# Fetches two steps ahead, mixes a unit later, gate logits behind the branch: a rearranged order in an RNN and mixture attention kernel

## The chip, the cores and the metric

The kernel runs on one core of one Trainium2 chip. The metric is the device time of one execution in microseconds (us); the time of a kernel is the median of its runs. TensorE is called PE, its weight loads PEld, VectorE DVE, ScalarE ACT, GpSimd POOL and SyncE SP. A letter q behind an engine's name in the profile means its sequencer.

## The reference, cut to what matters

Two layers, each with a residual, in float32, for 2 sequences of 2048 tokens of width 256:

```python
h_new = tanh(xi[t] + h @ Wh.T + bh)               # xi = layernorm(x) @ Wi.T + bi, over 2048 steps
x = x + hs
n = layernorm(x)                                  # 8 heads of 64, 5 experts, 2 of them chosen
gl_v = (n @ Ws).reshape(b, t, h, e);  wv = topk_mask(gl_v, 2) * sigmoid(gl_v)
xv = einsum('btd,edk->btek', n, Wv);  v = einsum('bthe,btek->bhtk', wv, xv)
attn = softmax(q * scale @ k.T) @ v               # q = n @ Wq, k = n @ Wk, per head
mask_o = topk_mask((n @ Wd).reshape(b, t, h, e), 2)
out = x + einsum('bthe,bthk,ekd->btd', mask_o, attn, Wo)
```

## The kernel before, in words

**Preparation.** The tokens are held as 16 chunks of 128 (`NCH` and `S` are 16). `measure` computes layer norm statistics on DVE, `turn_in` (L286) normalizes a chunk on POOL, transposes it on PE and copies it on ACT, and `project_in` (L297) multiplies it by Wi. In the loop at L318 `turn_in(c + 1)` is issued ahead of `project_in(c)`.

**The recurrence.** It is run as 128 short pieces side by side, twice (`run("a")` and `run("b")`, 13 and 16 steps); then DVE compares the pieces' ends with their starts (L504 to L509), and a branch on the count (L522, L523) repeats the run if they differ. `beside(s)` (L463) is issued behind each step of the second run: `turn_back` (L384) transposes the states of a chunk on PE and adds them to the residual `xt[c]` (ACT copies to `hv` and POOL adds, L395 and L396; for the last chunk DVE adds straight from PSUM, L392), and `x1d` is stored through SP. Behind the comparison stand `turn_norm` (L451) of the first eight chunks, and `logits` (L481) of chunks 0 to 3, with the matmul of the count, L517, in its middle. Its PSUM tile is of the pool `misc`, which has two buffers. After the branch come `queries(0, 0)`, `keys(0, 0)`, `logits(4)` and `turn_norm` of the other chunks.

**The attention.** There are 16 heads (2 sequences by 8), 4 blocks of 512 queries each: 64 units of four steps, `NT` = 256 steps in all. In step T, PE computes the scores (L634) of two key chunks, ACT copies them to SBUF (`stage`, L645), DVE keeps a running maximum (`largest`, L655). `LAG` = 6 steps later the maximum has been subtracted (`subtract`, L693, six of eight on POOL, the others on DVE), ACT has taken exponentials (L696), and PE multiplies by v (`products`, L706). A DMA issued by POOL adds pairs of probabilities (`fold`, L718).

**The order of the work beside it** is written out by hand. `at(table, T, f)` puts a call into step T, either `before` or `behind` the step's products; a later call for the same T comes later. What matters here:

- `fetch` (L605) loads the five experts' values of four chunks into `xq`, a tile with one buffer of 640 KB, by a DMA on SP's queue. `mix` (L610) multiplies it by the gates (L619), `mix_sum` (L623) sums over experts into `v` (L625). Each head has four parts. For heads after the first, `mix` stands at T, `fetch` at T - 1, `mix_sum` at T + 1 (L944 to L947). For the first head, `mix` reads values that were not fetched (`xf`).
- `experts` (L583) computes the second sequence's values while the first is in attention, two chunks in each of units 20 to 27, copies them (L588) and stores them on SP's queue (L589). The even chunk stands behind step 1 of a unit, the odd one before step 2.
- `gates` (L904) ranks the logits: ACT copies them to a tile of `misc` (`lg`, L223), DVE compares (`lt`, L236), and POOL counts ranks in five calls of `gates_go_on` (L241, L242, and L247 at the end for output gates). For the first sequence the output gates of part 0 and 1 stand at T = 4 and 10 (L925, L927). They are read first by `weigh` in `close` (L768), at step 12 for part 0 and 20 for part 1.

[...]

Of the kernel before, what the change touches and what calls it, by code (L numbers as in the profile page):

```python
# [14 lines left out]
P = 128  # L15
# [5 lines left out]
def rnn_then_switchhead_kernel(  # L21
# [98 lines left out]
    def misc(shape, nm):  # L120
        return ps_m.tile(shape, F32, tag="m", name=nm)
# [148 lines left out]
    with tc.tile_pool(name="prep", bufs=3) as pp, tc.tile_pool(  # L270
        name="lna", bufs=3
    ) as lnp, tc.tile_pool(name="ps_xi", bufs=3, space=PSUM) as ps_xi, tc.tile_pool(
        name="ps_t", bufs=3, space=PSUM
    ) as ps_t, tc.manual_schedule():
        norm_of, turned = {}, {}

        def measure(c0, n):
            mv = pp.tile([P, n * B, 2], F32, tag=f"mv{n}", name=f"mva{c0}")
            for c in range(c0, c0 + n):
                for b in range(B):  # L280
                    stats(lnp, mv[:, (c - c0) * B + b, :], xt[c][:, b, :], f"a{c}_{b}")
            neg, y = scales(lnp, mv, n * B, f"a{c0}")
            for c in range(c0, c0 + n):
                norm_of[c] = neg, y, (c - c0) * B

        def turn_in(c):  # L286
            neg, y, k = norm_of.pop(c)
            xn = pp.tile([P, B, D], F32, tag="xn", bufs=2, name=f"xn{c}")
            tp = ps_t.tile([P, KC, B, P], F32, tag="tp", name=f"tpa{c}")
            for b in range(B):  # L290
                normalize(xn[:, b, :], xt[c][:, b, :], neg, y, k + b)
                for kc in range(KC):
                    nc.tensor.transpose(tp[:, kc, b, :], xn[:, b, kc * P : (kc + 1) * P], ident)
            turned[c] = pp.tile([P, KC, B, P], F32, tag="xnT", bufs=2, name=f"xnT{c}")
            nc.scalar.copy(turned[c], tp)

        def project_in(c):  # L297
            xnT = turned.pop(c)
            for mc in range(KC):
                px = ps_xi.tile([P, B, P], F32, tag="px", name=f"px{c}_{mc}")  # L300
                for kc in range(KC):
                    nc.tensor.matmul(
                        px.rearrange("p b n -> p (b n)"),
                        lhsT=wi[:, kc, mc * P : (mc + 1) * P],
                        rhs=xnT[:, kc].rearrange("p b n -> p (b n)"),
                        start=kc == 0,
                        stop=kc == KC - 1,
                    )
                nc.scalar.activation(xi[:, mc, c], px, AF.Identity, bias=bsum[:, mc : mc + 1])

        groups, c0 = [], 0
        for n in (1, 1, 2, 3, 4, 5):
            groups.append((c0, n))
            c0 += n
        assert c0 == NCH
        measure(*groups.pop(0))
        nc.vector.tensor_tensor(bsum, bias[:, 0, :], bias[:, 1, :], ALU.add)
        for c in range(NCH):  # L318
            while groups and groups[0][0] <= c + 2:
                measure(*groups.pop(0))  # L320
            if c == 0:
                turn_in(0)
                project_in(0)
            if c + 1 < NCH:
                turn_in(c + 1)
            if c:
                project_in(c)


# [15 lines left out]
    ps_t = ctx.enter_context(ExitStack())  # L345
    pst = ps_t.enter_context(tc.tile_pool(name="ps_tb", bufs=2, space=PSUM))
    mv2 = [sp.tile([P, GC, 2], F32, tag=f"mv{g}", bufs=1, name=f"mvb{g}") for g in range(2)]
    tp_of, root_of = {}, {}

    def step(nm, s, prev, h, ps_h):  # L350
        for b in range(B):
# [29 lines left out]
                beside(s)  # L381
            prev = lambda kc, b, h=h: h[:, kc, b, :]

    def turn_back(c, nm, eng=None):  # L384

        tp = pst.tile([P, B, KC, P], F32, tag="tp", name=f"tpb{nm}{c}")
        for b in range(B):
            for kc in range(KC):
                nc.tensor.transpose(tp[:, b, kc, :], hs[:, kc, c, b, :], ident)
        tp = tp.rearrange("p b c d -> p b (c d)")  # L390
        if eng is nc.vector:
            nc.vector.tensor_tensor(xt[c], xt[c], tp, ALU.add)  # L392
        else:
            hv = sp.tile([P, B, D], F32, tag="hv", bufs=2, name=f"hv{nm}{c}")
            nc.scalar.copy(hv, tp)  # L395
            nc.gpsimd.tensor_tensor(xt[c], xt[c], hv, ALU.add)  # L396
        nc.sync.dma_start(out=x1d[c], in_=xt[c])

    def stats_back(c, nm):
# [63 lines left out]
    def beside(s):  # L463
        if s >= 1:
            turn_back(s - 1, "b")
        if s >= 2:
            stats_back(s - 2, "b")
        if s == GC + 2:
            root_of["todo"] = roots(mv2[0], GC, "b")
            next(root_of["todo"])  # L470
            next(root_of["todo"])
        if s == GC + 3:
            next(root_of["todo"])
            next(root_of["todo"])
        if s == GC + 4:
            *_, root_of[0] = root_of["todo"]
        if s >= GC + 4:
            c = 2 * (s - GC - 4)
            xn_of[c] = norm_back(c, "b", (nc.scalar, nc.gpsimd))

    def logits(c0, nm, between=None):  # L481

        pg = misc([P, 4, 2 * HE], f"pg{nm}{c0}")
        for c in range(c0, c0 + 4):
            for kc in range(KC):
                nc.tensor.matmul(
                    pg[:, c - c0, :],
                    lhsT=xn2T[:, kc, 0, c * P : (c + 1) * P],
                    rhs=wsd[:, kc, :],
                    start=kc == 0,  # L490
                    stop=kc == KC - 1,
                )
            if between and c == c0 + 1:
                between()
        nc.scalar.copy(gates_all[:, c0 : c0 + 4, 0, :], pg)

    with tc.tile_pool(name="ps_h", bufs=1, space=PSUM) as ps_h:

        with tc.manual_schedule():
            run("a", True, False, ps_h)  # L500
            run("b", False, True, ps_h, beside)
            N = KC * B * NS
            off = sp.tile([P, KC, B, NS], F32, tag="off", bufs=1, name="off")
            nc.vector.tensor_tensor(off, hs[:, :, S - 1], ends[:, :, :, 1:], ALU.subtract)  # L504
            good = sp.tile([P, KC, B, NS], F32, tag="good", bufs=1, name="good")
            nc.vector.tensor_scalar(good, off, TOL, None, ALU.is_le)
            nc.vector.scalar_tensor_tensor(good, off, -TOL, good, ALU.is_ge, ALU.mult)
            count = sp.tile([P, 1], F32, tag="count", bufs=1, name="count")
            nc.vector.tensor_reduce(count, good.rearrange("p c b n -> p (c b n)"), AX.X, ALU.add)  # L509
            turn_norm(0, xn_of.pop(0), "b")  # L510
            turn_back(S - 1, "b", nc.vector)
            for c in range(2, GC, 2):
                turn_norm(c, xn_of.pop(c), "b")
            pc = misc([1, 1], "pc")
            logits(
                0, "b",
                lambda: nc.tensor.matmul(pc, lhsT=count, rhs=ones, start=True, stop=True),  # L517
            )
            stats_back(EARLY - 1, "b")
            again = sp.tile([1, 1], I32, tag="again", bufs=1, name="again")  # L520
            nc.vector.tensor_scalar(again, pc, float(P * N) - 0.5, None, ALU.is_lt)
        flag = nc.values_load(again[0:1, 0:1], min_val=0, max_val=1)  # L522
        with tc.If(flag > 0):  # L523
            for c in range(S):
                load_x(c)
            with tc.For_i(0, NS - 1, 1):
                nc.vector.tensor_copy(ends[:, :, :, 1:], hs[:, :, S - 1])
                run("c", False, True, ps_h)
            for c in range(S):
                turn_back(c, "c")  # L530
                if c < EARLY:
                    stats_back(c, "c")
            *_, root_of[0] = roots(mv2[0], GC, "c")
            for c in range(0, GC, 2):
                turn_norm(c, norm_back(c, "c", pool2), "c")
            logits(0, "c")

    with tc.manual_schedule():

# [2 lines left out]
        for c in range(GC, S, 2):  # L542
            xn_of[c] = norm_back(c, "d", (nc.vector, nc.gpsimd))
        queries(0, 0)
        keys(0, 0)
        logits(4, "d")
        for c in range(GC, S, 2):
            turn_norm(c, xn_of.pop(c), "d")
    ps_t.close()
# [372 lines left out]
        at(behind, part, logits_first, HC + 4 * part)  # L922
    for part in range(2):
        at(behind, 1 + part, gates, 0, part, 0, True)
        at(behind, 4 + 6 * part, gates, 0, part, 1, False)  # L925
        for k in range(E):
            at(behind, 5 + 6 * part + k, gates_go_on)  # L927
    for i, (b, h) in enumerate(heads):
        T0 = i * H_T
        if i == 0:  # L930
# [8 lines left out]
        for part in range(4):  # L939
# [1 line left out]
                at(behind, (3, 5, 6, 7)[part], mix, i, part)  # L941
                at(behind, (3, 5, 6, 7)[part], mix_sum, i, part)
            else:
                T = max(T0 + U_T * (part - 3) + 2, LAG + 2)  # L944
                at(behind, T - 1, fetch, i, part)
                at(behind, T, mix, i, part)
                at(before, T + 1, mix_sum, i, part)  # L947
        if h == H - 3 and b + 1 < B:
# [158 lines left out]
```

## Time and profile before

| what | us |
|---|---|
| median of 3 runs (lowest, highest) | 1626.83 (1624.53, 1630.81) |
| the profiled execution: its time, its span | 1623.28, 1621.5 |
| PE, DVE, ACT, POOL busy | 1539.0, 1296.5, 1250.2, 1284.8 |
| attention starts (first copy of a score tile) | 135.0 |
| a unit of four steps, late in the span (four units from 1166.5 on) | 19.9, 21.5, 20.9, 20.6 |
| units 0 to 3 | 28.1, 29.3, 27.4, 21.0 |
| units 20 to 27 (584.8 to 782.3) | 197.5 in all |

Busy time of an engine over the whole span is an average over stages; what a change in one stage is worth is read from the windows of that stage. A unit is counted from the first copy L645 of its first step.

### The profile page before, as it was taken

How to read it: one execution, taken by the hardware profiler on the slowest of the kernel's cores; microseconds unless marked ns; L12 is line 12 of the kernel's file. 1: busy time of each engine (PE TensorE's matmuls, PEld its weight loads, DVE VectorE, ACT ScalarE, POOL GpSimd, SP SyncE). 2: the span in 40 equal slices, each digit the busy share in tenths (PEclk: the TensorE clock that was granted, in tenths of full speed). 3: DMA queues.
4: the chain of work that ended last, by engine and by line, in shares of the span. 5: the costliest groups of instructions: out<-in, count | busy, mean ns of one | idle time of the engine just before them, and what ended most of it. 6: DMA issues, size and time to landing. Idle time of an engine off the chain costs nothing.

```text
span 1621.5 us, 29233 instructions
## 1 busy us (share of the span) xinstructions
PE 1539.0 (95%) x11442; PEld 594.1 (37%) x11442; DVE 1296.5 (80%) x1807; ACT 1250.2 (77%) x1616; POOL 1284.8 (79%) x857
## 2 busy tenths in 40 slices
PE   6989899999999999998999999999999999999996
PEld 5974223333333333333333333333333333333333
DVE  7473789998988887777887768898888888988763
ACT  4664678888888888777887768888888888888862
POOL 3054688888888988888998768898889899998980
PEclk9999999999999999999999999999999999999999
DMA  5021368788888888677886767788888888889762
GB/s 161 1 106 37 106 141 193 176 188 173 178 172 172 173 168 172 139 166 143 180 182 156 174 148 178 168 169 174 169 172 169 178 160 177 168 174 186 153 134 86
DMA packets 86624, 252.27 MB, mean 156 GB/s; under 512 B 11920, under 2 KB 31184, under 8 KB 86480
## 3 DMA queue, kind: packets, MB, share of 16 engines
q0 software_dynamic: 43200, 163.60, 53.9%
q1 hardware_dynamic: 41648, 86.13, 17.6%
q8 instruction: 92, 1.51, 0.4%
q10 hardware_dynamic: 1632, 0.61, 0.1%
q14 instruction: 52, 0.43, 0.1%
HBM read 59.46 MB, written 50.33 MB: 68 GB/s over the span
## 4 chain that ended last, share of the span: by engine, by line
PE 64%; DVE 15%; DMA 6%; ACT 3%; issue 3%; POOL 1%; SPq 0%; DVEq 0%; ACTq 0%
PE s L634 23%; PE o L706 20%; DVE m L655 6%; PE d L727 6%; PE pq L159 4%; PE pk L140 3%; ACT p L645 3%; DMA xq<-xvd 2%; DMA p<-p 2%; PE pz L846 2%; DVE pro L772 2%; PE pt L683 2%; PE pm L668 1%; DVE p L693 1%; PE po L759 1%
## 5 line engine op out<-in xcount | busy, mean ns | idle before, releaser
L693 POOL TENSOR_TENSOR p<-p,top 128x1024 f32<-128x1024 f32 x381 | 1053.6, 3002 | 4.8 <-ACT top L686 4.6
L645 ACT COPY p<-s 128x1024 f32<-128x1024 f32 x512 | 511.0, 1011 | 161.4 <-DVE m L655 70.1
L696 ACT ACTIVATE p<-p 128x1024 f32<-128x1024 f32 x512 | 538.1, 1062 | 47.8 <-DVE p L693 38.1
L634 PE MATMUL s<-qs,k 64*128 64x512 f32 x1024 | 511.3, 617 | 7.7 <-ACT p L645 7.7
L634 PE MATMUL s<-q,k 64*128 64x512 f32 x1024 | 511.3, 617 | 6.7 <-ACT p L645 5.9
L706 PE MATMUL o<-p,v 128*32 128x512 f32 x4096 | 492.0, 597 | 8.5 <-DVE os L743 6.4
L655 DVE TENSOR_TENSOR m<-s,m 128x1024 f32<-128x1024 f32 x320 | 390.7, 1221 | 78.3 <-PE s L634 69.1
L718 POOL DMA_DIRECT2D p<-p x252 | 339.8, 1348 | 69.7 <-ACT p L696 22.9
L706 PEld LDWEIGHTS o<-p,v 128*32 128x32 f32 x4096 | 114.6, 109 | 297.2 <-issue 157.7
L634 PEld LDWEIGHTS s<-qs,k 64*128 64x128 f32 x1024 | 168.8, 185 | 145.3 <-issue 49.2
L634 PEld LDWEIGHTS s<-q,k 64*128 64x128 f32 x1024 | 168.8, 185 | 141.9 <-issue 49.6
L693 DVE TENSOR_TENSOR p<-p,pt 128x1024 f32<-128x1024 f32 x131 | 158.4, 1210 | 0.1
L727 PE MATMUL d<-p,ones 128*32 128x512 f32 x1040 | 151.5, 594 | 1.7 <-DMA p<-p 1.7
L655 DVE TENSOR_TENSOR m<-s,p 128x1024 f32<-128x1024 f32 x64 | 78.4, 1224 | 53.8 <-ACT p L645 53.4
L814 POOL DMA_DIRECT2D yd<-pro x48 | 43.3, 903 | 94.1 <-DVE pro L772 90.2
L619 DVE TENSOR_TENSOR xq<-xq,wp 128x1280 f32<-128x1280 f32 x60 | 89.2, 1487 | 28.3 <-DMA xq<-xvd 26.5
L772 DVE TENSOR_TENSOR pro<-po,mr 128x1280 f32<-128x1280 f32 (+1 forms) x67 | 95.9, 1431 | 2.7
L625 DVE TENSOR_REDUCE v<-xq 128x256 f32<-128x1280 f32 x60 | 88.6, 1476 | 0.0
L159 PE MATMUL pq<-xn2T,wq 128*32 128x512 f32 x512 | 66.8, 635 | 12.8 <-DVE xq L619 8.7
L727 PEld LDWEIGHTS d<-p,ones 128*32 128x32 f32 x1040 | 37.8, 110 | 91.9 <-issue 77.0
L140 PE MATMUL pk<-xn2T,wk 128*32 128x512 f32 x512 | 61.5, 598 | 0.7 <-ACT q L169 0.7
L673 DVE TENSOR_REDUCE mq<-pm 128x4 f32<-128x512 f32 x64 | 44.3, 692 | 19.2 <-PE pm L668 17.8
(175 smaller groups left out, 1472.4 us busy)
## 6 DMA issues: line engine op xcount, KB each, us to landing
p<-p POOLq DMA_DIRECT2D x252, 512.0 KB, 6.2
xq<-xvd SPq DMA_DIRECT2D x60, 640.0 KB, 5.2
yd<-pro POOLq DMA_DIRECT2D x48, 640.0 KB, 7.5
qs<-q SPq DMA_DIRECT2D x64, 128.0 KB, 2.7
yd<-pro SPq DMA_DIRECT2D x8, 640.0 KB, 4.1
y<-yd SPq DMA_DIRECT2D x8, 640.0 KB, 6.8
x<-in_x SPq DMA_DIRECT2D x16, 256.0 KB, 5.5
x1d<-x SPq DMA_DIRECT2D x16, 256.0 KB, 2.0
```

The lines of the kernel that those rows point to most:

```text
L140: nc.tensor.matmul(pk[at_col : at_col + 32], lhsT=wk[:, kc, h * DH + g : h * DH + g + 32], rhs=xc[:, kc, c0 // 2 : (c0 + HC) // 2, o, :], ...
L159: nc.tensor.matmul(pq[at_col : at_col + 32, :], lhsT=wq[:, kc, h * DH + g : h * DH + g + 32], rhs=xn2T[:, kc, b, n * QB : (n + 1) * QB], s ...
L619: nc.vector.tensor_tensor(xq, xq, wp.unsqueeze(2).to_broadcast([P, 4, DH, E]), ALU.mult)
L634: nc.tensor.matmul(ss[:, o, :], lhsT=k_of[i][half, c, :], rhs=q_of[i, n][o][half, :], start=True, stop=True,)
L645: nc.scalar.copy(p, ss)
L655: nc.vector.tensor_tensor(m, ss, ring[t - 1] if c == 1 else m, ALU.max)
L693: eng.tensor_tensor(p, p, top.unsqueeze(1).to_broadcast([P, 2, QB]), ALU.subtract)
L696: nc.scalar.activation(ring[t], ring[t], AF.Exp)
L706: nc.tensor.matmul(o_of[u][at_col : at_col + 32, :], lhsT=v_of[i][:, 2 * c + o, g : g + 32], rhs=ring[t][:, o, :], start=c == 0, stop=c == ...
L718: nc.gpsimd.dma_start(out=ring[t], in_=ring.pop(t + 1), accum_op=ALU.add)
L727: nc.tensor.matmul(den_of[u][32 * g : 32 * (g + 1), :], lhsT=ones32, rhs=ring[(t, t1)[g // 2]][:, g % 2, :], start=first, stop=last, tile_ ...
L772: nc.vector.tensor_tensor(dst, po[:, s : s + n, 0:DH].unsqueeze(2).to_broadcast([P, n, E, DH]), mr[:, s : s + n].unsqueeze(3).to_broadcast ...
```

## The change

Six edits, all of order and place:

1. `project_in(1)` is issued ahead of `turn_in(2)`.
2. `turn_back` only transposes and copies to `hv`, for the last chunk too; a new `add_back` adds. The sums of chunks 14 and 15 move to DVE, behind the comparison.
3. `logits(0)` moves from ahead of the branch to behind `queries(0, 0)`, and both `logits` take a PSUM tile of the pool of the transposes instead of `misc`.
4. `turn_norm(0)` follows the last `turn_back`.
5. The output gates of the first sequence move three steps on.
6. Mixes move four steps on (one unit), and each fetch stands two steps ahead of its mix instead of one.

```diff
-                project_in(0)
+            if c < 2:
+                project_in(c)
             if c + 1 < NCH:
                 turn_in(c + 1)
-            if c:
+            if c >= 2:
                 project_in(c)
...
-        tp = tp.rearrange("p b c d -> p b (c d)")
-        if eng is nc.vector:
-            nc.vector.tensor_tensor(xt[c], xt[c], tp, ALU.add)
-        else:
-            hv = sp.tile([P, B, D], F32, tag="hv", bufs=2, name=f"hv{nm}{c}")
-            nc.scalar.copy(hv, tp)
-            nc.gpsimd.tensor_tensor(xt[c], xt[c], hv, ALU.add)
+        hv_of[c] = sp.tile([P, B, D], F32, tag="hv", bufs=2, name=f"hv{nm}{c}")
+        nc.scalar.copy(hv_of[c], tp.rearrange("p b c d -> p b (c d)"))
+
+    def add_back(c, eng):
+
+        eng.tensor_tensor(xt[c], xt[c], hv_of.pop(c), ALU.add)
         nc.sync.dma_start(out=x1d[c], in_=xt[c])
...
         if s >= 1:
             turn_back(s - 1, "b")
+        if 1 <= s < S - 1:
+            add_back(s - 1, nc.gpsimd)
...
-        pg = misc([P, 4, 2 * HE], f"pg{nm}{c0}")
+        pg = pst.tile([P, B * D], F32, tag="tp", name=f"pgd{c0}")[:, : 4 * 2 * HE]
+        pg = pg.rearrange("p (c g) -> p c g", c=4)
...
-            turn_norm(0, xn_of.pop(0), "b")
-            turn_back(S - 1, "b", nc.vector)
-            for c in range(2, GC, 2):
+            turn_back(S - 1, "b")
+            for c in range(0, GC, 2):
                 turn_norm(c, xn_of.pop(c), "b")
             pc = misc([1, 1], "pc")
-            logits(
-                0, "b",
-                lambda: nc.tensor.matmul(pc, lhsT=count, rhs=ones, start=True, stop=True),
-            )
+            nc.tensor.matmul(pc, lhsT=count, rhs=ones, start=True, stop=True)
+            for c in (S - 2, S - 1):
+                add_back(c, nc.vector)
...
         queries(0, 0)
+        logits(0)
         keys(0, 0)
-        logits(4, "d")
+        logits(4)
...
-        at(behind, 4 + 6 * part, gates, 0, part, 1, False)
+        at(behind, 7 + 6 * part, gates, 0, part, 1, False)
         for k in range(E):
-            at(behind, 5 + 6 * part + k, gates_go_on)
+            at(behind, 8 + 6 * part + k, gates_go_on)
...
-                T = max(T0 + U_T * (part - 3) + 2, LAG + 2)
-                at(behind, T - 1, fetch, i, part)
+                T = T0 + U_T * (part - 2) + 2
+                at(behind, T - 2, fetch, i, part)
                 at(behind, T, mix, i, part)
                 at(before, T + 1, mix_sum, i, part)
```

## The prediction

> **What bounds the kernel now.** I read the page's first part, then its slices, the waits, and the windows of the stages touched.
>
> ```profile
> PE 1539.0 (95%) x11442; PEld 594.1 (37%) x11442; DVE 1296.5 (80%) x1807; ACT 1250.2 (77%) x1616; POOL 1284.8 (79%) x857
> ...
> DVE xq L619 <- DMA xq<-xvd: 26.5, 7, 6.2
> ...
> SPq L607 <- DVE v L625: 412.1, 38, 21.7
> ...
> SPq L589 <- ACT xw L588: 140.9, 14, 19.8
> ```
>
> PE is busy in 95% of the span, so most of it cannot shrink by a new order: only stages where PE stands idle, or does not yet set the pace, can. The waits (us in total, times, longest) name one: seven mixes wait 26.5 us for their fetch. SP's own waits say why it is seven: 38 fetches stand ready until `mix_sum` L625 frees the single `xq`, but in units 20 to 27 SP is held by the stores of `xw`, L589. The timeline of SP shows such a store right ahead of a fetch:
>
> ```profile
> 716.07 0.33 SPq L589 DMA_DIRECT2D xvd<-xw  x1
> 716.49 0.90 SPq L607 DMA_DIRECT2D xq<-xvd  x1
> ```
>
> The `mix_sum` before it ended at 704.79 + 1.48 = 706.3, 10 us before this fetch was issued. The worst of the seven, in the timeline (start, duration, in brackets the idle time of the engine ahead and what ended it):
>
> ```profile
> 749.21 1.49 DVE L619 TENSOR_TENSOR xq<-xq,wp 128x1280 f32<-128x1280 f32 x1 [6.18 <-DMA xq<-xvd]
> ...
> 750.84 3.15 PE L159 MATMUL pq<-xn2T,wq 128*32 128x512 f32 x16 [4.16 <-DVE xq L619]
> ```
>
> PE itself waits 4.16 us here, and its next 16 matmuls take 3.15 us where the chain of waits has 1.85 us for the same 16 at 251.00. The windows of units 26 and 27 (length, busy us of PE, PEld, DVE, ACT, POOL, clock, DMA share, GB/s), and of unit 1:
>
> ```profile
> 729.70:758.80 29.10, 24.94 (x184) 8.43 (x177) 19.88 (x26) 19.98 (x26) 23.40 (x16) 0.94 0.71 150
> 758.80:782.30 23.50, 23.15 (x182) 8.33 (x184) 18.02 (x21) 18.78 (x23) 21.25 (x20) 1.00 0.70 148
> ...
> 163.10:192.40 29.30, 21.72 (x172) 7.86 (x170) 21.27 (x25) 16.76 (x22) 18.22 (x14) 0.94 0.29 90
> ```
>
> In units 1 and 2 PE is idle 7.6 and 3.7 us; from 175 to 211 the chain of waits runs mostly through DVE. From unit 3 on PE sets the pace.
>
> **What the Trainium skill says.** "TensorE: Matmul & The Clock Gate", What's actually happening: PE's clock falls to half after an idle window of about 3.4 us and needs as long to recover. The trace agrees: clock 0.94 in the window with the 4.16 us wait. "Runtime: NRT & Kernel Launch", Instruction fetch mechanics: a taken branch whose target is not loaded waits for a fetch of instructions. It fits PE's 4.10 us idle behind L523 (DVE: 1.51); so that stop should stay. "SBUF — State Buffer", Who interferes with whom: a DVE instruction with both inputs in SBUF contends with a POOL instruction reading SBUF. That concerns the moved `add_back`, but POOL has nothing to do beside it then; no run here separates it.
>
> **The change part by part.** The sum is made against the profiled execution, 1623.28 us (span 1621.5), which lies 3.55 below the median of 1626.83; I apply the difference to the median.
>
> *Fetch at T - 2.* No instruction is added. In the changed order each fetch comes on SP ahead of both `xw` stores of its unit, not between them. Then it is issued when `mix_sum` ends, as in the undisturbed units, where 5.2 us to landing (median) leave slack before a mix about 13 us later (782.06 to 795.45). All seven waits should go. What that is worth is PE's idle time, not 26.5: the windows of units 20 to 27 sum to 197.5 us with PE busy 185.04, so 12.5 idle; 3.15 - 1.85 = 1.3 more is the slow clock. Undisturbed units late in the span still show (82.9 - 81.76)/4 = 0.3 idle, so 2.3 stay. Ceiling: 12.5 + 1.3 - 2.3 = 11.5. POOL comes next: it is busy 22.83 and 23.40 in units 23 and 26, with gate ranks among the subtractions, so those cannot go under about 23.4. I take **-9**, range -12 to -4. On SP the fetch passes the even `xw` store, and in the output units a store L855 and a load of `z`; these now stand behind 640 KB. The stores come 10 us after `mix_sum`, so nothing there is held; a `z` load may land later where DVE already waits (15.9 us in 7 times): 0, bound -1 to +3.
>
> *Mixes a unit on.* In steady units the same steps hold the same work, for another part: 0. DVE's queue loses one mix at step 8 (0.17 + 1.49 + 1.48 = 3.1 us, at 196.45, 196.66 and 202.61), in the stretch where DVE is the chain: -3.1. At the end a mix moves into unit 60 or 61, where PE fills the time and DVE has 2 to 4 us idle: 0. The last part's sum is read two steps behind, the others' five or more, so lateness is not near. The fetch for each moves as well; the first, on an idle queue, costs nothing.
>
> *Output gates three steps on.* Leaving step 4: PE waits 2.27 us at 168.31 for `lt`, which holds a `misc` buffer; the ACT copy of `top` ends at 166.66, so PE gains about 1.6, and DVE follows PE there. Leaving step 10: DVE's 1.63 us wait for `lg` and 1.06 of `lt` at 209.03: -2.7. Arriving at step 7, DVE again the chain: the four `lt` 1.1 and a wait for `lg` behind an exponential of ACT, 1.3: +2.4. Arriving at step 13 in a unit bound by PE: 0 to 2.7, taken +0.5. POOL's rank work (10 instructions, 0.6 to 1.3 us each, per part) shifts along. Its last, L247, now stands in step 12 behind the sixth subtraction of unit 1; before, that ended at 220.16, so with 1.32 us L247 would end near 221.5, and its reader on DVE came at 223.95. If the stage runs 5 us earlier this slack of 2.4 is used up: POOL had 5.4 us of gaps between 195 and 220 to catch up. I count 1 us lost.
>
> So the start of the attention: -3.1 - 1.6 - 2.7 + 2.4 + 0.5 + 1 = **-3.5**, range -7 to +1.
>
> *Logits behind the branch.* 16 matmuls, 1.96 us in the chain (pgd), move onto PE's path behind the branch. They cover the 0.69 us that PE waited for ACT's q. The transposes behind them now share two buffers with both logits: one more wait for the copy, about 0.3. The flag: before, DVE wrote it at 116.64 after waiting 1.17 for the count's matmul. Now DVE goes from the count (114.31) through two sums of 0.66 (like `off`), statistics 0.6, flag 0.15: about 116.35 to 116.5, 0.3 earlier. Together 1.96 - 0.69 + 0.3 - 0.3 = **+1.2**, range -0.5 to +2.5. ACT's copy of chunk 15 (0.57) and the order of `turn_norm` lie under the comparison, 3.8 us on DVE.
>
> *project_in(1) earlier.* 3.05 us of PE work moves into the 2.74 us idle ahead of 17.59. But chunk 4 is ready on POOL only at 22.67 + 0.55 = 23.2, PE took it at 23.66, and chunk 7 again at 29.97 against 30.16: **-0.2**, range -0.5 to 0.
>
> Sum: -9 - 3.5 + 1.2 - 0.2 = -11.5, so 1626.8 - 11.5 = **1615**.
>
> **Rivals.**
>
> *The gain of the expert units is not cashed.* POOL is busy 167.72 of those 197.5 us and folds and subtractions are in its queue; the waits removed could reappear at L693 or L696. Then -3 there, and the start gives -1: about **1624**. For it: DVE idles 5 us per unit there and still PE lost only 12.5. Against: units 28 and 29 run at 20.6 with POOL nearly full.
>
> *The fetches do not come earlier*, since `mix_sum` holds `xq`. For most of the 60 that is so and gives 0; for the seven the queue shows the contrary. It would leave -3.5 + 1.0: **1624** too.
>
> *Slower: the fetch at the head of SP holds the stores behind it.* SP now meets the fetch first and stands until `mix_sum` ends; `xw` has two buffers, so a late store stops ACT's L588, then the `misc` tile, then PE. It decides only where `mix_sum` ends later than the store could go; today it ends about 10 us earlier. If a step (6 us) were lost in each of four of the eight units, 24 - 11.5 = +12.5: about **1639**; from two such units on the gain is gone.
>
> **How the numbers follow.** One profile and run differ here by up to 0.4%; 0.5% (8.1 us) is about what can be told from no change. Forecast 0.68, mostly below 1618.7, some of it just above; the two rivals of small gain 0.26; slower 0.06. Faster by over 0.5%: 0.66; within: 0.28; slower: 0.06. The range runs from the far bounds, -21, to the small-gain rivals: 1605 to 1626.
>
> **What would show it.** Right: no wait of DVE for xq in units 20 to 27, each fetch issued at the end of L625, those units near 187 us in all, unit 26 near 24; units 0 to 2 about 3 us shorter, `lt` at steps 7 and 13; attention starting near 136; PE's stop at the branch still about 4 us. Wrong: a wait of L768 for POOL's L247, of L693 or L696 in the expert units, of `z`, or of SP's L589 behind L607; or a start of the attention later than 138.

## The result, and the profile after

The changed kernel takes 1618.94 us (median of 9 runs, 1613.51 to 1620.83) against 1626.83 for the kernel before in the same job: a ratio of 0.9944, 95% interval 0.9927 to 0.9961 (one median divided by the other gives 0.9952). By the medians that is 7.9 us less. The forecast was 1615, with 1605 to 1626 as its range. The profiled execution took 1618.95 us, its span 1617.2.

In the waits of SP's queue (us in total, times, longest) the stores of `xw` hold SP for less time, and more of its fetches stand ready until `mix_sum` frees `xq`:

```profile
SPq L607 <- DVE v L625: 430.4, 42, 21.8
...
SPq L589 <- ACT xw L588: 101.2, 14, 10.8
```

DVE's waits have no line for `xq <- DMA` any more (26.5 us in seven times before). The timeline of the changed kernel shows why, in the fetch for the mix of unit 25, among the expert units:

```profile
698.32 1.48 DVE L625 TENSOR_REDUCE v<-xq 128x256 f32<-128x1280 f32 x1
...
699.82 0.33 SPq L607 DMA_DIRECT2D xq<-xvd  x1
...
709.59 4.43 SPq L589 DMA_DIRECT2D xvd<-xw  x2
...
713.71 1.49 DVE L619 TENSOR_TENSOR xq<-xq,wp 128x1280 f32<-128x1280 f32 x1
```

`mix_sum` ends at 699.80 and the fetch is issued at 699.82; both stores follow 10 us later, and the mix has no idle time in front of it. The windows of units 1, 2, 26 and 27 (columns as in the prediction), and of units 20 to 27 as a whole:

```profile
166.58:192.50 25.92, 20.48 (x172) 7.23 (x168) 20.32 (x23) 16.80 (x23) 16.09 (x10) 1.00 0.37 109
192.50:215.46 22.96, 21.44 (x152) 6.75 (x152) 19.62 (x22) 18.21 (x23) 21.02 (x19) 1.00 0.51 97
721.96:745.87 23.91, 23.02 (x180) 7.42 (x176) 18.60 (x25) 19.61 (x25) 23.91 (x16) 1.00 0.81 172
745.87:768.66 22.79, 22.79 (x178) 8.19 (x176) 18.33 (x22) 18.79 (x22) 21.31 (x20) 1.00 0.75 159
...
584.31:768.66 184.35, 182.01 (x1452) 64.38 (x1449) 150.89 (x181) 152.33 (x189) 167.25 (x124) 1.00 0.81 171
```

Unit 1 went from 29.30 to 25.92 us, unit 26 from 29.10 to 23.91, where POOL is now busy in all of it; the clock is 1.00 in each of these lines. But the gains in units 0 to 3 (7 us) and 20 to 27 (13 us) are more than twice the 7.9 that the kernel gained. The table shows where the rest is: by stage, in us from the windows, for every kernel that was run. "Start" is the first copy L645, "tail" everything from unit 63 on.

| kernel | edits it has | start | units 0-3 | 4-19 | 20-27 | 28-35 | 36-62 | tail | span |
|---|---|---|---|---|---|---|---|---|---|
| before | none | 135.0 | 105.7 | 344.0 | 197.5 | 197.9 | 557.7 | 83.7 | 1621.5 |
| e1 | none | 138.4 | 104.4 | 344.1 | 200.2 | 197.9 | 559.0 | 84.5 | 1628.4 |
| after | all | 138.4 | 98.5 | 347.3 | 184.3 | 198.3 | 564.6 | 85.6 | 1617.2 |
| e2 | all | 134.6 | 98.6 | 347.5 | 184.3 | 198.7 | 564.2 | 85.6 | 1613.5 |
| e3 | fetch at T - 2 | 135.4 | 104.4 | 342.6 | 184.3 | 198.7 | 557.5 | 83.4 | 1606.4 |
| e4 | fetch ahead of the store | 137.8 | 105.6 | 343.2 | 184.3 | 198.9 | 557.9 | 84.4 | 1612.1 |
| e5 | mixes | 134.3 | 101.3 | 343.7 | 199.0 | 199.3 | 564.7 | 83.2 | 1625.4 |
| e6 | gates | 135.4 | 99.9 | 343.0 | 197.5 | 198.9 | 558.7 | 82.8 | 1616.3 |
| e7 | branch (2 to 4) | 137.4 | 106.0 | 346.3 | 196.9 | 198.7 | 561.0 | 84.6 | 1630.9 |
| e8 | all but mixes | 134.8 | 100.0 | 346.1 | 184.3 | 199.0 | 560.0 | 84.5 | 1608.7 |
| e9 | fetch, gates | 137.5 | 99.9 | 343.2 | 184.3 | 200.4 | 558.4 | 83.6 | 1607.3 |
| e10 | as e8, matmuls back in the dead branch | 134.4 | 99.9 | 342.6 | 184.2 | 199.6 | 557.9 | 82.8 | 1601.5 |
| e11 | mixes of the last head | 135.5 | 104.4 | 343.2 | 199.8 | 197.6 | 560.9 | 84.1 | 1625.4 |
| e12 | all, two mended | 136.1 | 98.5 | 343.4 | 184.4 | 199.9 | 565.1 | 82.9 | 1610.3 |

Two things are read from it at once. The start of the attention lies anywhere from 134.3 to 138.4 with no relation to the edits: the unchanged kernel alone gave 135.0 and 138.4. And the changed kernel is 3 us slower in units 4 to 19, 5 to 7 in 36 to 62 and 1 to 2 in the tail than the two profiles of the kernel before (before, e1), and it repeats this in both of its own (after, e2). The forecast had put all of that at nothing.

### The profile page after: what moved, and what is told of

Its sections match the earlier page's. It is cut to its first block, busy times and chain, and to the rows that moved or that the text cites. A ratio compares the mean times of both kernels' runs of the same rounds, so it can differ in the third digit from the quotient of the medians.

```text
span 1617.2 us, 29233 instructions
## 1 busy us (share of the span) xinstructions
PE 1540.3 (95%) x11442; PEld 593.7 (37%) x11442; DVE 1297.6 (80%) x1808; ACT 1251.0 (77%) x1617; POOL 1285.5 (79%) x856
## 4 chain that ended last, share of the span: by engine, by line
PE 67%; DVE 12%; DMA 6%; ACT 3%; issue 2%; POOL 2%; SPq 0%; DVEq 0%; ACTq 0%; POOLq 0%
PE s L634 23%; PE o L706 20%; PE d L727 6%; DVE m L655 5%; DMA p<-p 4%; PE pk L140 4%; PE pq L159 3%; PE pz L846 2%; ACT p L645 2%; PE pt L683 2%; DVE pro L772 2%; PE pm L668 1%; POOL p L693 1%; PE po L759 1%; DVE p L693 1%
## 5 line engine op out<-in xcount | busy, mean ns | idle before, releaser
L645 ACT COPY p<-s 128x1024 f32<-128x1024 f32 x512 | 511.0, 1011 | 152.8 <-DVE m L655 66.9
L718 POOL DMA_DIRECT2D p<-p x252 | 341.4, 1355 | 60.0 <-PE o L706 21.5
L727 PE MATMUL d<-p,ones 128*32 128x512 f32 x1040 | 153.1, 593 | 5.1 <-DMA p<-p 5.0
L727 PEld LDWEIGHTS d<-p,ones 128*32 128x32 f32 x1040 | 37.5, 110 | 97.2 <-issue 76.8
L159 PE MATMUL pq<-xn2T,wq 128*32 128x512 f32 x512 | 63.3, 612 | 6.3 <-DVE rtd L427 6.3
L673 DVE TENSOR_REDUCE mq<-pm 128x4 f32<-128x512 f32 x64 | 44.3, 692 | 18.3 <-PE pm L668 16.9
```

The costliest lines, as they stand in the source:

```text
L159: nc.tensor.matmul(pq[at_col : at_col + 32, :], lhsT=wq[:, kc, h * DH + g : h * DH + g + 32], rhs=xn2T[:, kc, b, n * QB : (n + 1) * QB], s ...
L645: nc.scalar.copy(p, ss)
L718: nc.gpsimd.dma_start(out=ring[t], in_=ring.pop(t + 1), accum_op=ALU.add)
L727: nc.tensor.matmul(den_of[u][32 * g : 32 * (g + 1), :], lhsT=ones32, rhs=ring[(t, t1)[g // 2]][:, g % 2, :], start=first, stop=last, tile_ ...
```

## The experiments

Ratios are to the kernel before on the same chip in the same job, with 95% intervals.

**The noise, and the change again.** e1 is the kernel before with a blank line in it:

```diff
     ps_t = ctx.enter_context(ExitStack())
+
     pst = ps_t.enter_context(tc.tile_pool(name="ps_tb", bufs=2, space=PSUM))
```

> The kernel before, unchanged but for an empty line: it measures what two profiles of one program differ by, stage by stage. In the profiles shown so far the changed kernel loses 3.3 us in units 4 to 19 and 6.9 us in units 36 to 62, where its order of work is that of before with another part of v. Theory 'variation': these stages differ by several us between two executions of one program, so here they should lie up to some 5 us away from 344.0 and 557.7. Rival 'collision': the moved fetches and mixes cost there; then this profile repeats 344.0 and 557.7 within 1 us. Ratio to the kernel before 1.000 within 0.002; units 20 to 27 near 197.5 with seven waits for xq in either case.

Measured: 0.9994 (0.9981 to 1.0007). Its profile again has 26.5 us of waits for `xq` in seven times, and its stages differ from those of before by 1.4 us at most, apart from the start (3.4) and units 20 to 27 (2.7).

e2 is the changed kernel a second time, without an edit.

> The changed kernel again. Both theories: ratio 0.9944 within 0.002, units 20 to 27 near 184 us, attention starting near 138. 'Variation': units 4 to 19 and 36 to 62 move by several us from 347.3 and 564.6. 'Collision': they stay within 1 us of these. On the cold clock behind the branch, where 16 matmuls of logits took 3.6 us for the 1.96 of before: if the PE's pause of 6.3 us makes it, it is seen again.

Measured: 0.9935 (0.9915 to 0.9956). Its stages from unit 0 on agree with those of the first profile within 0.4 us; its attention started 3.9 us earlier. So the slower steady units are no variation between executions, and the late start in the first profile of the changed kernel is one. The slow matmuls behind the branch are not seen again either: the first 16 of `logits` took 3.70 us in the first profile and 2.01 here, although PE had stopped for 6.54 us here and for 6.32 there.

**The fetch.** e3 is the kernel before with the earlier fetch alone:

```diff
-                at(behind, T - 1, fetch, i, part)
+                at(behind, T - 1 if (i, part) == (1, 1) else T - 2, fetch, i, part)
```

> The kernel before with the fetches alone two steps ahead of their mixes (one fetch of the second head stays one step ahead, because its buffer is still read there). Theory 'queue': the fetch no longer stands behind the store of xw on SP, all seven waits of DVE for xq go, units 20 to 27 take about 184 us instead of 197.5, 13 less, and the whole is 0.992 of before, more than all six edits together bring. Rival 'share': POOL or the moved mixes make part of the 184, and the fetch alone leaves them near 190, ratio 0.996. Rival 'collision' in the steady units: ratio about 1.0, units 36 to 62 near 564.

Measured: 0.9931 (0.991 to 0.9952), and 184.3 us in units 20 to 27. This one line brings as much as all six edits together.

e4 leaves the fetch one step ahead of its mix and only puts it in front of the store of that step:

```diff
-                at(behind, T - 1, fetch, i, part)
+                at(before, T - 1, fetch, i, part)
```

> The kernel before with each fetch in the same step as before, one ahead of its mix, but in the step's list that is issued ahead of the products instead of behind them: on SP it then stands ahead of the step's store of xw, which is behind them. Theory 'queue': it is the place in SP's queue alone, so units 20 to 27 take about 184 us as with two steps, waits for xq 0, ratio 0.992. Rival 'distance': a step (6 us) of time is needed, since landing takes 5 to 10 us; then waits for xq remain, some 10 us of the 26.5, and units 20 to 27 stay above 190.

Measured: 0.9926 (0.9906 to 0.9946), 184.3 us again. Its timeline reads like that of the changed kernel:

```profile
679.82 0.32 SPq L607 DMA_DIRECT2D xq<-xvd  x1
...
689.32 4.44 SPq L589 DMA_DIRECT2D xvd<-xw  x2
...
693.66 1.49 DVE L619 TENSOR_TENSOR xq<-xq,wp 128x1280 f32<-128x1280 f32 x1
```

So the number of steps between a fetch and its mix is not what counts. Its place in SP's queue, ahead of a store that is not ready, is the whole of the gain.

**Which edit costs the steady units.** Four kernels, one edit or group each. e5 moves the mixes alone:

```diff
-                T = max(T0 + U_T * (part - 3) + 2, LAG + 2)
+                T = T0 + U_T * (part - 2) + 2
```

> The kernel before, with mixes and sums four steps later and each fetch still one step ahead of its mix (edit 6 without the earlier fetch). The changed kernel loses about 3.4 us in units 4 to 19 and 6.5 in units 36 to 62 against the kernel before, and gains 7 in units 0 to 3. Theory 'mixes': the moved mixes do both. Then units 0 to 3 take about 100 us (105.7 before), units 4 to 19 347, units 36 to 62 564, the waits for xq in units 20 to 27 stay (197 to 200), and the time is 1.003 to 1.006 of before. Theory 'gates or branch': units 36 to 62 stay at 558, units 4 to 19 at 344, and the time is 0.997 to 1.000 with units 0 to 3 about 3 us shorter.

Measured: 1.0005 (0.9993 to 1.0017). Units 0 to 3 gain 3.1 to 4.5 us (against e1 and the kernel before), units 36 to 62 lose 6 to 7, most of it in 61 and 62 (44.5 us together against 39.8); units 4 to 19 lose nothing. So the mixes are one cause, and not the only one.

e6 moves the output gates alone:

```diff
-        at(behind, 4 + 6 * part, gates, 0, part, 1, False)
+        at(behind, 7 + 6 * part, gates, 0, part, 1, False)
...
-            at(behind, 5 + 6 * part + k, gates_go_on)
+            at(behind, 8 + 6 * part + k, gates_go_on)
```

> The kernel before, with the output gates of the first sequence three steps on (edit 5 alone). Theory 'mixes': the steady units are as before (344, 558), units 0 to 3 are 0 to 3 us shorter, ratio 0.998 to 1.000. Theory 'gates': the shift of misc tiles puts everything behind it on another buffer; units 4 to 19 take 347 and units 36 to 62 564, ratio 1.002 to 1.006.

Measured: 0.9953 (0.9941 to 0.9966), better than either theory said. Units 0 to 3 take 99.9 us, and the steady units are as before. Of DVE's waits in units 1 to 3, this line of the kernel before

```profile
DVE lt L236 <- ACT lg L223: 2.3, 2, 1.6
```

has become, in e6,

```profile
DVE lt L236 <- ACT lg L223: 0.2, 1, 0.2
```

and in the same units PE's wait of 2.3 us for `lt` is gone and that of 2.7 us for `xq` down to 0.4.

With these two stops goes something that the prediction did not count: the slow clock behind them. In the kernel before the clock is 0.94 in units 1 and 2, in e6 it is 1.00. What that is worth in unit 1 can be read from e1, where the same stop of 2.27 us happened to leave the clock at 1.00. The 48 matmuls behind the stop, in the kernel before and in e1 (its blank line moves line numbers by one):

```profile
168.31 4.80 PE L574 MATMUL pvf<-wv,xn2T 128*32 128x320 f32 x48 [2.27 <-DVE lt L236]
171.66 3.44 PE L575 MATMUL pvf<-wv,xn2T 128*32 128x320 f32 x48 [2.27 <-DVE lt L236]
```

The difference, 1.4 us, is that of unit 1 in the two profiles (29.25 and 27.88). In unit 2 PE is busy for 23.67 us at clock 0.94 in the kernel before and for 21.97 at clock 1.00 in e3, where the same stop is 2.67 us long: 1.7 us.

e7 has edits 2 to 4 alone, the part around the branch (the diff in the section on the change, without `project_in`, gates, mixes and fetch).

> The kernel before, with edits 2 to 4 alone: sums of the last chunks on DVE behind the comparison, logits behind the branch with a tile of the transposes' pool, turn_norm(0) later. The prediction: +1.2 us, ratio 1.000 to 1.002, the attention starting 1 us later than in the null run of the kernel before, units as before. Theory 'branch': two misc tiles fewer turn the parity of the rotation of misc for the whole attention, and units 36 to 62 take 564: ratio 1.005 to 1.007.

Measured: 1.0022 (1.0009 to 1.0035). The ratio lies just above the range of the prediction and below that of the theory. Units 4 to 19 lose 2 us, units 36 to 62 lose 2 to 3, although no instruction of theirs was touched. From the last matmul of the recurrence to the first copy L645, the kernels with the new order at the branch take 24.5 to 27.5 us (six profiles), those with the old one 24.4 to 28.1 (eight).

e8 is the changed kernel with its mixes back:

```diff
-                T = T0 + U_T * (part - 2) + 2
-                at(behind, T - 2, fetch, i, part)
+                T = max(T0 + U_T * (part - 3) + 2, LAG + 2)
+                at(behind, T - 1 if (i, part) == (1, 1) else T - 2, fetch, i, part)
```

> The changed kernel with its mixes back at the steps of the kernel before, fetches still two steps ahead of them (edits 1 to 5 and the earlier fetch). Theory 'mixes': units 20 to 27 take 184.3, units 4 to 19 344 and 36 to 62 558, units 0 to 3 about 102: span about 1606, ratio 0.988 to 0.992, better than both kernels. Theory 'gates or branch': units 36 to 62 stay at 564 and 4 to 19 at 347, ratio 0.993 to 0.996.

Measured: 0.9916 (0.9901 to 0.993). The ratio is one that theory 'mixes' allows, but the stages lie between the theories, as they must with two causes: 36 to 62 fall from 564 to 560, and units 4 to 19 keep their 346.

**What the branch edit does to units far behind it.** Single units tell. In all the kernels up to here with edits 2 to 4 (both profiles of the changed kernel, e7, e8), units 12, 14, 46 and 56 take 21.8 to 22.2, 24.6 to 25.2, 22.1 to 22.8 and 21.8 to 22.2 us; in all without, 21.3, 23.1 to 23.6, 21.5 to 21.7 and 20.3 to 20.5. In unit 56 of e8, PE waits 0.9 us in L727 for a `fold`. What differs there is not in the program's order.

The edit also takes `logits(0, "c")` out of the body of the branch, which is never executed here (the diff of the change leaves this line out): 16 matmuls and 16 weight loads fewer in PE's program. The page of e8 lists a DMA queue q8 of kind "instruction" with 91 packets of 16 KB; PE's 22,884 matmuls and weight loads are 89.4 times 256. "Runtime: NRT & Kernel Launch", Instruction fetch mechanics, says that each engine's instructions arrive in blocks of 16 KiB, 256 instructions, and calls the cost of a block mostly hidden. With 32 instructions fewer, the blocks arrive at other moments. The packets of q8 show it: in units 12, 14, 46 and 56 one comes 2.7 to 6.3 us after the unit's start in the four profiles with the edit, and not before 14.6 us in all that leave the code in its place.

e10 is e8 with that code back where it is never executed:

```diff
             for c in range(0, GC, 2):
                 turn_norm(c, norm_back(c, "c", pool2), "c")
+            logits(0)
```

> e8_no_mix with one call of logits(0) put into the branch that is not taken: nothing that is executed changes, only 16 matmuls and their weight loads come back into the PE program at the place from which the change removed them. Theory 'instruction fetch': the branch edit cost its 3 to 5 us in steady units because the PE program behind it begins 32 instructions earlier and so PE's blocks of instructions are loaded at other moments, in units 12, 14, 46 and 56 at 3 to 6 us from the unit's start, where they fall on a fold; with the 16 matmuls back these units take 21.3, 23.4, 21.5 and 20.4 again (22.2, 24.7, 22.8 and 22.0 in e8), units 4 to 19 343, 36 to 62 558, ratio about 0.989. Theory 'buffers': the parity of the misc buffers is what costs (it stays turned here): nothing changes, units 4 to 19 346, 36 to 62 560, ratio 0.991 to 0.992.

Measured: 0.9901 (0.9883 to 0.9919); the intervals of e8 and e10 overlap, so the verdict rests on the units. Units 12, 14, 46 and 56 take 21.3, 23.4, 21.5 and 20.5 us, units 4 to 19 342.6, 36 to 62 557.9: those of the kernels without edits 2 to 4. A fifth unit, 16, goes the same way, from 22.5 us in e8 to 21.5 in e10, with its block at 5.8 and at 19.5 us (in the kernel before it takes 22.9 without an early block, which is not explained). The rotation of the `misc` buffers is in e10 what it is in e8, so the rival falls. The windows of units 12 and 56 in e8,

```profile
403.46:425.63 22.17, 21.45 (x146) 6.96 (x148) 19.74 (x32) 17.66 (x20) 20.16 (x13) 1.00 0.86 173
1379.22:1401.26 22.04, 21.17 (x142) 6.85 (x140) 18.37 (x22) 17.67 (x20) 19.86 (x13) 1.00 0.85 171
```

and in e10:

```profile
402.44:423.71 21.27, 20.76 (x146) 6.96 (x148) 19.75 (x32) 17.62 (x21) 19.49 (x13) 1.00 0.85 173
1375.35:1395.86 20.51, 20.51 (x142) 6.84 (x140) 18.37 (x22) 17.63 (x20) 18.73 (x13) 1.00 0.90 180
```

The same counts of instructions on PE, DVE and POOL, the same busy time on DVE, and PE with 0.9 us of idle time in e8's unit 56 and none in e10's. PE's busy time differs too, by 0.7 us in each pair. In unit 56 that is L727: a fold that lands late parts its eight matmuls into two fours, and four alone take as long as eight together. In e8, then in e10:

```profile
1385.87 1.03 PE L727 MATMUL d<-p,ones 128*32 128x512 f32 x4
1387.77 1.05 PE L727 MATMUL d<-p,ones 128*32 128x512 f32 x4 [0.87 <-DMA p<-p]
...
1381.99 1.43 PE L728 MATMUL d<-p,ones 128*32 128x512 f32 x8
```

From the first to the last of the eight that is 2.95 us against 1.43, the whole of the 1.5 us by which the unit is longer.

The DMA view of the first 10 us of unit 56 (queues: packets, MB, share; issues: KB, median us to landing) in e8:

```profile
q8 instruction: 1, 0.02, 1.2%
...
p<-p POOLq DMA_DIRECT2D x3, 512.0 KB, 9.2
xq<-xvd SPq DMA_DIRECT2D x1, 640.0 KB, 6.4
```

and in e10, which has no line of q8 there:

```profile
p<-p POOLq DMA_DIRECT2D x3, 512.0 KB, 7.8
xq<-xvd SPq DMA_DIRECT2D x1, 640.0 KB, 4.7
```

1.2% of 16 engines' 10 us is 2 us of one engine. Where this block of 16 KB falls among them, the fetch lands 1.7 us later and the folds 1.4. "DMA: Bandwidth & Descriptors", Why a DMA increments its semaphore by 16 and not by 1, says that a transfer is complete only when every engine it was spread over has reported; a block that occupies one of them would then delay the whole. That fits, but no run here shows which engine carried the block. Nor does every early block cost: in unit 55 of e8 one came 5.4 us after the start, and the unit took 20.95 us; in the kernel before it came at 19.7 us, and the unit took 20.89. And unit 44 has the early block in the kernels without the edit: at 2.8 us in the kernel before, which takes 21.2 us there, and at 5.9 us in e8, which takes 20.5.

**What the mixes do at the end.** In the changed kernel units 61 and 62 take 22.05 and 20.47 us, in the kernel before 19.88 each. SP's timeline for units 60 and 61 of the kernel before (unit 61 starts at 1498.08),

```profile
1477.44 0.33 SPq L607 DMA_DIRECT2D xq<-xvd  x1
...
1492.22 0.52 SPq L793 DMA_DIRECT2D y<-yd  x1
1492.79 0.44 SPq L838 DMA_DIRECT2D z<-x1d  x1
1493.34 0.37 SPq L793 DMA_DIRECT2D y<-yd  x1
```

and of the changed one (unit 61 starts at 1489.02):

```profile
1468.16 0.33 SPq L607 DMA_DIRECT2D xq<-xvd  x1
1481.72 0.47 SPq L170 DMA_DIRECT2D qs<-q  x1
1482.24 0.59 SPq L171 DMA_DIRECT2D qs<-q  x1
1488.80 0.33 SPq L607 DMA_DIRECT2D xq<-xvd  x1
1489.22 0.38 SPq L793 DMA_DIRECT2D y<-yd  x1
1489.65 0.42 SPq L838 DMA_DIRECT2D z<-x1d  x1
1490.18 1.09 SPq L793 DMA_DIRECT2D y<-yd  x1
```

Before, the last fetch had long been issued, and the loads of `y` (640 KB each) and `z` went out 5.9 us ahead of unit 61. Now a fetch stands ahead of them on SP and waits for `mix_sum` until 1488.8; it holds them 6.3 us, and 2.0 MB start together as the unit begins. In the first 14 us of unit 61 the folds take 10.3 us to land (median) where they took 7.3, and PE waits for them, with the eight matmuls of L727 parted again (timeline of the changed kernel, idle time in brackets):

```profile
1495.66 1.03 PE L727 MATMUL d<-p,ones 128*32 128x512 f32 x4
1497.25 1.05 PE L727 MATMUL d<-p,ones 128*32 128x512 f32 x4 [0.57 <-DMA p<-p]
...
1508.28 1.05 PE L727 MATMUL d<-p,ones 128*32 128x512 f32 x4 [0.95 <-DMA p<-p]
```

e11 moves the mixes of the last head alone:

```diff
-                T = max(T0 + U_T * (part - 3) + 2, LAG + 2)
+                T = max(T0 + U_T * (part - 3 + (i == len(heads) - 1)) + 2, LAG + 2)
```

> The kernel before with the mixes of the last head alone moved four steps later (its last mix then stands in unit 61). Theory 'collision at the end': its last fetch of 640 KB is then issued together with the loads of y and z (L793, L838) of the last output chunks in unit 61, the fold of that unit lands late and PE waits in L727: units 61 and 62 take 2 to 5 us more than 19.88 each in sum, everything else as before, 1.001 to 1.003. Theory 'steady cost': a mix moved by a unit costs in every unit a little; then units 61 and 62 stay within 0.5 us and the ratio is 1.000.

Measured: 1.003 (1.0018 to 1.0042). Units 61 and 62 take 21.78 and 20.47 us, 2.5 more in sum; the rest of the 5 us in the ratio is not located. In unit 61 SP's fetch again stands ahead of the loads (issued at 1498.84, the loads from 1499.27 on), and PE waits 1.4 us in L727 for a fold. The collision is shown; that a moved mix costs nothing elsewhere is not.

**Versions without the two costs.** e9 takes only what gained, the fetch of e3 with the gates of e6 (both diffs above).

> The kernel before with the earlier fetch and the output gates three steps on (edit 5 and the fetch part of edit 6), the mixes and the branch as before. If the parts add up, units 0 to 3 take about 100 us, 4 to 19 343, 20 to 27 184.3, 36 to 62 558, the tail 83: a span near 1601 where the attention starts at 135.4, ratio 0.985 to 0.989, faster than the changed kernel by 8 to 11 us. If the gains of gates and fetch lie on the same path, or what is gained at the start is waited for later, ratio 0.990 to 0.994.

Measured: 1609.06 us, 0.9898 (0.9879 to 0.9917). The interval lies below that of the first run of the changed kernel and meets that of its repeat at the edge (0.9917 and 0.9915). By the ratios this version is 6 to 7.5 us faster than the changed kernel, where 8 to 11 were expected. The stages add up as forecast (99.9, 343.2, 184.3, 558.4); the ratio lies just above the range of the first case, and in the profile the start (137.5 for 135.4) and the stage of units 28 to 35 (200.4 for 198.7 and 198.9 in e3 and e6) are 2.1 and 1.5 us longer.

e12 tried to mend the changed kernel instead: the dead matmuls of e10, and the last head's mixes spread so that the last stands in unit 60:

```diff
+            logits(0)
...
-                T = T0 + U_T * (part - 2) + 2
+                T = T0 + U_T * (part - 2) + 2 - (part + 1) * (i == len(heads) - 1)
```

> The changed kernel with two small edits: logits(0) put into the branch that is not taken (16 matmuls that are never executed), and the last head's mixes at 3, 2, 1 and 0 steps later than before instead of 4 each, so that the last one stands in unit 60. If the two causes found so far are the whole of what the changed kernel loses in steady units, units 0 to 3 take 98.5 us, 4 to 19 343, 20 to 27 184.3, 36 to 62 558, with units 12, 14, 46, 56, 61 and 62 at 21.3, 23.4, 21.5, 20.4, 19.9 and 19.9: span near 1601, ratio 0.988 to 0.991. If the moved mixes cost something in every unit as well, 36 to 62 stay at 560 or more and the ratio at 0.991 to 0.993.

Measured: 0.9918 (0.9899 to 0.9936). Units 12, 14, 46, 56, 61 and 62 are as forecast (21.3, 23.4, 21.7, 20.6, 19.9, 19.9), but 36 to 62 take 565.1: units 58 to 60 lose 5.9 us against e10. Where the spread puts a mix at the head of unit 59, PE waits for it:

```profile
PE po L760 <- DVE xq L620: 1.8, 1, 1.8
```

The windows show clock 0.50 behind that wait, and unit 59 takes 24.76 us. The mixes two steps into their units show no such wait. With units 58 to 60 as in e10, 36 to 62 would take 559.2, 1.2 us above e10. e5 points the same way: its units 36 to 60 take 520.2 us, where the seven kernels with neither a moved mix nor the cost of the branch edit take 517.7 to 518.9. So the moved mixes may cost 1 to 2 us over these units; one profile each is too little to call it shown.

## Why the prediction was right, and where it was not

The time lies in the range and the sign held; 1618.94 is just above the 1618.7 below which most of the forecast lay. The sum was 3.6 us too good: 11.5 forecast, 7.9 measured. That it came so near is in part luck. By the stages, the fetch and units 0 to 3 gained about 8 us more than forecast, and stages that the forecast had put at nothing or at +1.2 cost about 12. Two terms were too small, and two that stood at nothing were not nothing.

- **Fetch at T - 2, -9.** It is -13.2 (197.5 to 184.3; e1 has 200.2 there). The mechanism is the forecast one, and PE's idle time came out as worked out: 184.35 - 182.01 = 2.3 left. The mis-sized term is the ceiling: PE's busy time fell by 3.1 (185.05 to 182.01), not 1.3. The slow matmuls L159 gave 1.4 of it, as counted. What was left out is L727 with about 1.3, most of it because in the kernel before a late fold in unit 25 parts its eight matmuls into fours of 1.03 and 1.05 us (at 724.0 and 726.0), where eight together take 1.04. And the 2.5 us held back for POOL were not needed: unit 26 ended at 23.91, as POOL's limit had it, but the others had room.
- **Units 0 to 3, -3.5 in the sum, and the gates in it.** They gained 7 (6 against e1). The gates had been put at -0.4 (-1.6, -2.7, +2.4, +0.5, +1.0); they are worth 4.5 to 5.8 (e6 against e1 and the kernel before). One step that failed is the sum itself: it took PE's two stops and left out the half clock behind them, 1.4 us in unit 1 and 1.7 in unit 2, although the window of unit 1 that the prediction shows has clock 0.94. The other is the +2.4 for arriving at step 7 and the +1 for POOL. With the clock set aside, units 1 and 2 gain about 3.3 us (27.88 in e1 and 25.70 in e3 to 25.90 and 24.36 in e6), where the terms of these units sum to 0.9, and to 4.3 without those two: by this estimate about 1 us of the 3.4 came. DVE still waits 7.4 us for PE's scores in units 1 to 3 of the changed kernel, so there was room for the `lt` (this is argued, no run has it apart); and no wait for L247 appeared. The +0.5 at step 13 is there (unit 3: 20.96 to 21.52).
- **The mixes in units 0 to 3, -3.1 of that sum.** This fits e5, where they move alone (3.1 to 4.5), but not the changed kernel: beside the moved gates they bring only 1.4 (100.0 in e8, 98.5 to 98.6 with the mixes). The gains overlap, and the sum added them.
- **Logits behind the branch, +1.2.** At the start no cost can be seen: the flag comes 5.4 to 5.6 us behind the recurrence's last matmul instead of 7.1 to 8.3, much more than the 0.3 worked out. PE's stop at the branch grew to 6.1 to 6.6 us (2.8 to 4.1 with the old order) instead of staying at 4, but only because no logits fill its beginning any more: PE's branch instruction itself lasts 3.4 to 4.0 us in every profile, and PE goes on 10.3 to 10.9 us behind the recurrence's last matmul instead of 11.6 to 13.3. Later it did cost: 2 to 3.5 us in each of two stages, by the placing of PE's instruction blocks, which the prediction did not think of. The prediction counted executed instructions only; the edit removed some that are never executed.
- **Mixes a unit on, "in steady units 0, at the end 0".** The end was wrong, +2.8 us in units 61 and 62; in the steady units 1 to 2 us may be missing (e5, e12). The step that failed is "PE fills the time and DVE has 2 to 4 us idle": DVE was indeed idle, but the mix brings a fetch, and the fetch held SP's loads. This is the mechanism of the rival "Slower", a fetch at the head of SP that holds what is behind it, at one place that the rival did not look at. The expert units, where it looked, showed nothing of it.
- **The `z` loads, 0 (-1 to +3).** DVE's wait for them rose from 15.9 to 18.1 us, and the tail by 2; but e1, with the order of before, has 18.3 and 84.5. Kernels without the mixes moved have 82.8 to 84.6 us there, e5 83.2 and e11 84.1: that part is not settled.
- **project_in(1) earlier, -0.2.** No run has this edit alone, and a start that differs by 4 us between executions cannot show it.
- **The start later than 138 as a sign of failure.** A bad sign: the kernel before reaches 138.4 by itself.
- **A reading.** DVE's idle time in the expert units is 5.9 us a unit, (197.5 - 150.26)/8, not 5; no term rests on it.

In sum, with e2, whose start is like that of before: -0.4 start, -7.1, +3.5, -13.2, +0.8, +6.5 and +1.9 make -8.0, its span against 1621.5.

## What to carry to other kernels

A queue that issues DMAs in order, as SP's does here, is a resource to plan: a transfer whose condition is met late holds all behind it, so each issue belongs in the order of the times at which the conditions come true, and a moved step must be checked against what stands behind its DMA, to the last unit. Take a change of many edits apart stage by stage and edit by edit: here one line brought as much as six edits, and two of the six paid part of it back. Where steady stages change by a few us with no edit near, look at the DMA queues, the instruction queue among them, before calling it noise; the same program again tells the two apart. And price a stop of PE together with the slow clock that may follow it.

## What the runs showed that was not expected

Code that is never executed moved the time of units up to over a millisecond later, by 5.5 us in all (units 4 to 19 and 36 to 62: 906.1 us in e8, 900.6 in e10).

A fold that lands late costs more than the wait for it, since it parts matmuls that otherwise run together: eight of L727 take 1.04 us, and the two fours take 1.03 and 1.05.

PE's clock fell after shorter stops than the prediction's page has it. "TensorE: Matmul & The Clock Gate", What's actually happening, speaks of an idle window of about 3.4 us; in e5, unit 61, PE was busy from 1510.53 to 1515.20, idle for 2.13 us and then at half clock, as the windows show (PE's busy time second, clock third from the end):

```profile
1510.53:1515.20 4.67, 4.67 (x28) 1.33 (x28) 4.27 (x6) 4.09 (x5) 4.67 (x4) 1.00 1.06 212
1515.20:1517.33 2.13, 0.01 (x2) 0.00 (x1) 2.08 (x2) 0.63 (x1) 2.13 (x4) 0.98 1.05 208
1517.33:1519.20 1.87, 1.87 (x6) 0.21 (x6) 0.00 (x0) 0.00 (x0) 1.87 (x3) 0.50 0.65 127
```

The stops of 0.57 and 0.95 us in unit 61 of the changed kernel had no such effect: four matmuls of L727 took 1.05 us behind each, 1.92 behind the stop of 2.13. The length of the stop does not decide alone: behind the same 2.27 us in unit 1 the clock fell in the kernel before and not in e1.
